# Dilation: the ScalarE place of the sign that makes each pattern

## The chip, the cores and the metric

The kernel runs on one core of a Trainium2 chip. The metric is the device time of the whole program in microseconds (us); the number given for a kernel is the median of several runs. Engines are named as the profile names them: PE is TensorE, DVE is VectorE, ACT is ScalarE, POOL is GpSimd, SP is the engine that issues most of the transfers.

## The reference, cut to what matters

Sixteen graphs of 1024 nodes with 128 features pass through two graph layers. Layer 0 is three times `h = hW + b; cos = nh nh^T; h = (adj * cos) h`. Layer 1 needs a thinned adjacency first, which is a sequential scan over the rows of each graph:

```python
def step(carry, n):
    row = carry[n]
    num = sum(row)
    sf = where(num > 10, (num + 1) // 2, 1)
    rank = cumsum(row)
    rm = row & (rank % sf == 0) & (mask[n] != 0) & (num > 1)
    carry = carry.at[n].set(row & ~rm)
    carry = carry.at[:, n].set(carry[:, n] & ~rm)
keep = scan(step, adj > 0);  adj_d = adj * keep
```

The kernel calls this scan "dilation". Three message-passing steps with batch statistics follow on `adj_d`, and do not concern the change.

## The kernel before, in words

The program has two halves in time. In the first (up to about 1530 us in the profile), layer 0 and the dilation run side by side; in the second, layer 1 runs.

**Layer 0** is a Python generator, `layer0()`. It issues small units of work and yields each unit's estimated PE time: `products` (PE products `pg` L344, multiplied on DVE by the adjacency into `ew`, L353 and L356), `turn` (PE transposes `gt` L373, copied back on ACT, L374), `sums` and `sums_back` (PE, L384 and L398), transposes of the adjacency (`pt_a` L260 on PE, copied by ACT into `adjA`, L261), features, squares for the norms (`hS` L319 on ACT), and so on.

**The dilation** works on blocks. A block `(k, half)` is one strip of 128 rows in eight of the sixteen graphs, so there are 16 blocks, done one after the other. Each block has three phases:

- `loads()`, once for each of the eight graphs `i`: SP brings a strip `an` of the adjacency (two buffers, L585); ACT makes the pattern, a row of ones and zeros in f16, with `Sign` (L587) and then `Relu` in place, which also sums the row (L588); DVE writes the left part of the pattern (L594) from `an` and from what was kept before. At every fourth graph PE transposes the four diagonal tiles (`pdt`, L608), ACT copies them (`dT`, L610), PE forms `pT` (L614 to L616) and ACT copies that into `T` (L618).
- `rounds()`: DVE starts with `Z` from `T` (L632 or L635), then alternates with PE some two to six times, and ends with ACT copying `E` (L722).
- `scans()`: DVE subtracts `E` from the patterns (L732); then for each graph DVE runs a scan of 1024 elements (L741) over the pattern, ACT takes an absolute value (`Abs`, L751), DVE compares (`kp`, L762), and POOL sends the row out (L763).

The patterns live in a ring `patt` of ten slots for blocks of eight. Pattern `i` of the next block, for `i` from 2 on, takes the slot of pattern `i-2` of the present block, and so may only be written when the scan of that pattern is over. Patterns 0 and 1 of the next block take the slots that the block before the present one used for its patterns 6 and 7.

**The code's order.** `dilation()` issues the loads of the next block among the scans of the present one: after each scan, one load. Every phase yields weights (0.8 a load, 2.5 a scan, 0.8 an `Abs`), and the driving loop issues layer-0 units in proportion until they have caught up, about 2 us of PE estimate for each unit of weight. In the code the order round scan `i` is therefore: scan `i`; layer-0 units; sign and relu `i` of the next block (and after `i` = 3 and 7 the `pdt`, `dT`, `pT`, `T` of its four graphs); layer-0 units; `Abs` `i-1`; layer-0 units; scan `i+1`.

**The order on an engine.** The framework that builds the program does not keep the code's order on an engine. It places instructions by its own estimate of when their operands are ready, so that an instruction may be put ahead of others that the code issued before it. `tc.keep_in_program_order(ins)` takes this away for one instruction: `ins` is not placed ahead of the last instruction that the code issued on the same engine before it. It adds no wait on hardware; it acts on the order of the queue alone. In the kernel before, the scans on DVE (L741) and the `Abs` on ACT (L751) are pinned in this way; the signs are not.

Of the kernel before, what the change touches and what calls it, by code (L numbers as in the profile page):

```python
# [11 lines left out]
AF = mybir.ActivationFunctionType  # L12
# [4 lines left out]
P = 128  # L17
# [29 lines left out]
def tile_adj_preln_d2(  # L47
# [40 lines left out]
    nc = tc.nc  # L88
# [111 lines left out]
    with ExitStack() as actx:  # L200
# [362 lines left out]
        def dilate(k, half, exact):  # L563
# [6 lines left out]
            def pattern(i):  # L570
                return patt[:, (at0 + i) % SLOTS, :]
# [9 lines left out]
            def loads():  # L581
                for i in range(BH):
                    b = half * BH + i
                    an = poold.tile([P, N], F32, tag="an", name=f"an{nk}_{i}")
                    nc.sync.dma_start(an, adj[b, cols, :])  # L585
                    on = pattern(i)[:, 2 + k * P :]
                    nc.scalar.activation(on, an[:, k * P :], AF.Sign)  # L587
                    nc.scalar.activation(on, on, AF.Relu, accum_out=rest[:, i : i + 1])  # L588
                    if k:
                        pk = poold.tile([P, NCH - 1, P], F16, tag="kl", name=f"kl{nk}_{i}")  # L590
                        nc.sync.dma_start(
                            pk[:, :k, :].rearrange("p j q -> p (j q)"), keep_d[b][: k * P, cols], transpose=True
                        )
                        nc.vector.scalar_tensor_tensor(  # L594
                            pattern(i)[:, 2 : 2 + k * P],
                            an[:, : k * P],
                            0.0,
                            pk[:, :k, :].rearrange("p j q -> p (j q)"),
                            ALU.is_gt,
                            ALU.mult,  # L600
                            accum_out=left[:, i : i + 1],
                        )
                    if i % GT == GT - 1:
                        four = range(i - GT + 1, i + 1)
                        bs_ = slice(i - GT + 1, i + 1)
                        pdt = ps_sm.tile([P, GT, P], F16, tag="sm", name=f"pdt{nk}_{i}")
                        for n, ii in enumerate(four):
                            nc.tensor.transpose(pdt[:, n, :], pattern(ii)[:, diag], ident16)  # L608
                        dT = poold.tile([P, GT, P], F16, tag="dT", bufs=1, name=f"dT{nk}_{i}")
                        nc.scalar.activation(dT, pdt, AF.Copy)  # L610
                        nc.vector.tensor_scalar(rbias[:, bs_], rest[:, bs_], 2.0, -2.0, ALU.mult, ALU.add)
                        pT = ps_sm.tile([P, GT, P], F32, tag="sm", name=f"pT{nk}_{i}")
                        for n, ii in enumerate(four):
                            nc.tensor.matmul(pT[:, n, :], lhsT=dT[:, n, :], rhs=upto, start=True, stop=False)  # L614
                            nc.tensor.matmul(pT[:, n, :], lhsT=pattern(ii)[:, diag], rhs=off, start=False, stop=False)
                            nc.tensor.matmul(pT[:, n, :], lhsT=ident16, rhs=after, start=False, stop=True)  # L616
                        for n, ii in enumerate(four):
                            nc.scalar.activation(T[:, ii, :], pT[:, n, :], AF.Identity, bias=rbias[:, ii : ii + 1])  # L618
                    yield 0.8
# [105 lines left out]
            def scans():  # L725
# [9 lines left out]
                for i in range(BH + 1):  # L735
# [28 lines left out]
                    yield False, 0.8  # L764

            return loads(), rounds(), scans()

        units0 = layer0()
# [448 lines left out]
```

## Time and profile before

| | |
|---|---|
| median of three runs | 2819.08 us (2816.39 to 2822.73) |
| the profiled execution | 2820.68 us |
| its span, first to last instruction | 2818.8 us |
| mean granted PE clock | 0.985 |
| busy in the span: PE, DVE, ACT, POOL | 2649.9, 1947.1, 1426.5, 477.6 us |
| sign L587 | 128 instructions, 293 / 686 / 1069 ns (least, median, most), from 17.1 to 1415.7 us |
| relu L588 | 128 instructions, 294 / 676 / 1082 ns, and 187 ns each for reading the sum |
| scan L741 | 128 instructions, 2282 ns (median), from 79.5 to 1511.1 us |
| last row of the dilation sent (L763) | 1521.3 us |

The span is divided at about 1530 us: before it, layer 0 and the dilation share the engines; after it comes layer 1. A "busy" figure counts the time in which an engine executed something; a wait is the idle time of an engine just before an instruction, with the instruction whose end allowed it to go on. Sizes differ between the signs because block `k` signs only the columns from `128k` on: 1024 elements a row at first, 128 in the last blocks.

### The profile page before, as it was taken

The page shows a single profiled execution, that of the slowest core. Times are in us where ns is not written, and L with a number is a line of the kernel's source. Part 1 is how long each engine was busy: PE and PEld are TensorE (multiplying, and loading weights), DVE is VectorE, ACT ScalarE, POOL GpSimd, SP SyncE. Part 2 cuts the span into 40 slices and gives each one's busy share as a digit, 9 for nine tenths or more (in the row PEclk, how much of TensorE's full clock was granted, in tenths as well). Part 3 has the DMA queues.
Part 4 walks back from the last instruction along what each step waited for, and adds up shares of the span by engine and source line. Part 5 has one row for each costly group of instructions (what it writes and reads, how often), then busy time and mean ns, then how long its engine had stood idle before and what let it go on. Part 6 is the DMA issues. An engine that isn't in the chain of part 4 may idle for free. (4 is left out here: it accounts for less than half of the span.)

```text
span 2818.8 us, 51980 instructions
## 1 busy us (share of the span) xinstructions
PE 2649.9 (94%) x18803; PEld 2193.2 (78%) x18803; DVE 1947.1 (69%) x4943; ACT 1426.5 (51%) x4097; POOL 477.6 (17%) x616
## 2 busy tenths in 40 slices
PE   6999999999999999999999999999989999999997
PEld 4666666676776676666676778888889999899997
DVE  3778778788888788889886467777762333456556
ACT  6757667558556566466454333343333334333334
POOL 3112112012012111121121012222220101010101
PEclk9999999999999999999999999999999999999999
DMA  8437347258366476386354069999976666576774
GB/s 283 135 128 241 99 159 240 75 159 245 85 201 173 101 226 186 95 254 182 93 178 162 1 234 386 402 402 387 402 297 214 203 216 201 188 238 228 234 237 135
DMA packets 382233, 585.22 MB, mean 208 GB/s; under 512 B 85200, under 2 KB 266448, under 8 KB 381968
## 3 DMA queue, kind: packets, MB, share of 16 engines
q1 hardware_dynamic: 343280, 425.28, 48.2%
q0 software_dynamic: 38688, 156.53, 14.8%
q8 instruction: 151, 2.47, 0.4%
q14 instruction: 114, 0.93, 0.1%
HBM read 403.44 MB, written 163.58 MB: 201 GB/s over the span
## 5 line engine op out<-in xcount | busy, mean ns | idle before, releaser
L890 PE MATMUL agg<-hw,aT 128*128 128x128 f32 (+1 forms) x6144 | 743.5, 277 | 8.2 <-DVE aT L995 7.3
L890 PEld LDWEIGHTS agg<-hw,aT 128*128 128x128 f32 x6144 | 713.4, 193 | 13.6 <-DVE aT L995 9.7
L344 PE MATMUL pg<-nhT 128*128 128x512 f32 (+3 forms) x1152 | 454.7, 497 | 40.4 <-DVE ew L356 39.1
L384 PE MATMUL po<-ew,hS 128*128 128x512 f32 (+3 forms) x1152 | 453.3, 497 | 8.1 <-ACT hTo L407 3.7
L356 DVE TENSOR_TENSOR ew<-pg,adjA 128x768 f32<-128x768 f32 (+3 forms) x528 | 423.6, 826 | 5.0 <-PE pg L344 5.0
L398 PEld LDWEIGHTS po<-ew,hS 128*128 128x128 f32 x2688 | 339.5, 193 | 39.1 <-issue 36.8
L398 PE MATMUL po<-ew,hS 128*128 128x128 f32 x2688 | 367.5, 277 | 1.2 <-ACT ew L374 1.2
L374 ACT ACTIVATE ew<-gt 128x512 f32<-128x512 f32 (+1 forms) x480 | 208.5, 464 | 245.3 <-PE gt L373 238.0
L741 DVE TENSOR_TENSOR_SCAN rank<-patt 128x1024 f16<-128x1024 f16 x128 | 294.9, 2305 | 0.1
L344 PEld LDWEIGHTS pg<-nhT 128*128 128x128 f32 x1152 | 187.9, 192 | 131.7 <-issue 89.3
L384 PEld LDWEIGHTS po<-ew,hS 128*128 128x128 f32 x1152 | 195.2, 193 | 99.8 <-issue 64.6
L373 PEld LDWEIGHTS gt<-ident,ew 128*128 128x128 f32 x1344 | 168.5, 143 | 100.7 <-issue 75.4
L373 PE MATMUL gt<-ident,ew 128*128 128x128 f32 x1344 | 212.3, 277 | 4.8 <-PEq L824 2.5
L948 POOL TENSOR_TENSOR o<-o,rn 128x512 f32<-128x512 f32 x93 | 108.5, 1167 | 638.3 <-DVE rn L942 627.6
L353 DVE TENSOR_TENSOR ew<-pg,adjA 128x128 f32<-128x128 f32 x384 | 108.1, 282 | 156.6 <-PE pg L344 117.3
L864 DVE TENSOR_TENSOR own<-pw,bs 128x256 f32<-128x256 f32 x192 | 81.4, 424 | 155.5 <-ACT hw L863 155.4
L862 PE MATMUL pw<-wrx,hT 128*128 128x256 f32 x768 | 179.7, 388 | 9.2 <-ACT hT L1065 8.4
L862 PEld LDWEIGHTS pw<-wrx,hT 128*128 128x128 f32 x768 | 145.1, 194 | 31.3 <-ACT hT L1065 9.2
L1013 ACT ACTIVATE aT<-pta 128x512 f32<-128x512 f32 (+3 forms) x160 | 71.3, 467 | 187.4 <-PE pta L1012 181.9
L751 ACT ACTIVATE rank<-rank,fin 128x1024 f16<-128x1024 f16 x128 | 146.7, 1151 | 36.3 <-DVE rank L741 35.6
L940 ACT ACTIVATE own<-o 128x128 f32<-128x128 f32 x378 | 112.7, 301 | 99.7 <-DVE o L919 99.5
L321 POOL TENSOR_TENSOR hS<-hN,rn 128x1024 f32<-128x1024 f32 x48 | 102.5, 2136 | 355.5 <-DVE rn L157 226.0
(169 smaller groups left out, 3930.6 us busy)
## 6 DMA issues: line engine op xcount, KB each, us to landing
an<-in_adj_dram SPq DMA_DIRECT2D x128, 512.0 KB, 4.3
keep<-kp POOLq DMA_DIRECT2D x128, 256.0 KB, 2.9
kb<-keep SPq DMA_DIRECT2D x128, 256.0 KB, 5.5
aT<-adT SPq DMA_DIRECT2D x32, 960.0 KB, 4.7
aT<-adT SPq DMA_DIRECT2D x32, 832.0 KB, 4.6
aT<-adT SPq DMA_DIRECT2D x32, 704.0 KB, 4.2
aT<-adT SPq DMA_DIRECT2D x32, 576.0 KB, 3.4
xb<-in_x_dram SPq DMA_DIRECT2D x31, 512.0 KB, 5.2
```

Source lines behind the costliest of these rows:

```text
L344: nc.tensor.matmul(pg[:, :n, :].rearrange("p c q -> p (c q)"), lhsT=self.nhT[:, q * P : (q + 1) * P], rhs=self.nhT[:, (q + c) * P : (q + c ...
L356: nc.vector.tensor_tensor(both[0][:, :, off, :], pg[:, own:n, :].unsqueeze(1).to_broadcast([P, 2, n - own, P]), both[1][:, :, off, :], ALU ...
L373: nc.tensor.transpose(pt[:, i, :], ew[:, at + i, :], ident)
L374: nc.scalar.activation(ew[:, at : at + n, :], pt[:, :n, :], AF.Copy)
L384: nc.tensor.matmul(self.po[:, c * P : (c + n) * P], lhsT=self.hS[:, q, :], rhs=ew[:, c - q : c - q + n, :].rearrange("p c q -> p (c q)"), ...
L398: nc.tensor.matmul(self.po[:, q * P : (q + 1) * P], lhsT=self.hS[:, q + n, :], rhs=ew[:, NCH - 1 - q + n, :], start=False, stop=closes and ...
L741: nc.vector.tensor_tensor_scan(rank, pt[:, 1 : N + 1], pt[:, 2:], 0.0, ALU.add, ALU.add)
L751: nc.scalar.activation(rank, rank, AF.Abs, bias=shift[:, i : i + 1], scale=1.0 if exact else -1.0)
L862: nc.tensor.matmul(pw[:, i, :], lhsT=hT[:, 2 * h + i, :], rhs=wrx[:, l, :], start=True, stop=True)
L890: nc.tensor.matmul(self.place(c), lhsT=aT[:, blk, :], rhs=self.hw[:, source, :], start=source == 0 and c % self.ga == 0, stop=ends(c, source),
L940: nc.scalar.activation(sq, o, AF.Square, accum_out=ss[:, c : c + 1])
L948: nc.gpsimd.tensor_tensor(self.o[:, hc, :], self.o[:, hc, :], rn.unsqueeze(2).to_broadcast([P, CPH, D]), ALU.mult)
```

## The change

One instruction is pinned: the `Sign` that makes a pattern. Nothing is computed differently, and no instruction is added or removed.

```diff
                     nc.sync.dma_start(an, adj[b, cols, :])
                     on = pattern(i)[:, 2 + k * P :]
-                    nc.scalar.activation(on, an[:, k * P :], AF.Sign)
+                    tc.keep_in_program_order(nc.scalar.activation(on, an[:, k * P :], AF.Sign))
                     nc.scalar.activation(on, on, AF.Relu, accum_out=rest[:, i : i + 1])
```

In the changed program a sign stands on ACT behind the ACT instruction that the code issued last before it: mostly a copy of a layer-0 unit (L374, L261), sometimes a square root (L155), the closing copy of a layer (L407) or the relu of the pattern before. The relu itself is not pinned, but reads what the sign wrote.

## The prediction

> **What bounds the kernel now.** I read the page first, then a table of busy time by stretch, the waits of ScalarE, the rows of the sign and of the transposes that read its pattern, and the timeline of one block. The dilation lies in the first 1525 us, so only that part can move. The busy time in it, and in two stretches of block 7, its scans (718 to 787) and the rounds after it (786 to 811), with columns PE, PEld, DVE, ACT, POOL:
>
> ```profile
> 70.00:1525.00 1455.00, 1373.47 (x8692) 1002.29 (x8690) 1200.24 (x2829) 904.79 (x2413) 254.57 (x317) 0.99 0.55 161
> ```
>
> ```profile
> 718.00:787.00 69.00, 66.21 (x387) 47.43 (x386) 56.26 (x104) 40.72 (x113) 9.05 (x9) 1.00 0.38 106
> ...
> 786.00:811.00 25.00, 24.53 (x185) 18.24 (x183) 22.17 (x62) 10.74 (x26) 2.17 (x4) 1.00 0.38 125
> ```
>
> PE is busy 94%, DVE 82%, ACT 62%. PE sets the pace; it loses 81.5 us in all there, and more of it in scans (2.8 of 69 us) than in rounds (0.5 of 25). ACT has room: what it idles costs only through those who wait for it. So what does ACT wait for, and who waits for its sign?
>
> ```profile
> ACT patt L587 <- DVE rank L741: 93.5, 73, 2.9
> ...
> ACT rank L751 <- DVE rank L741: 35.6, 20, 4.4
> ...
> ACT patt L587 <- DMA an<-in_adj_dram: 13.3, 6, 4.5
> ```
>
> ```profile
>   PEld pg L344: 2.1, 1
>   PE pt_a L260: 0.6, 1
> ```
>
> The first row is what the change is about: 73 of 128 signs stand at the head of ACT until a scan frees their slot, 93.5 us together. The second fence, the sign's own row, shows how little hangs on the sign directly: PE 0.6 us. Now the timeline from 768 to 789 us, block 7's last scans, with two signs, scan 7, a layer-0 copy, `pdt`, `dT`, and the start of the next rounds:
>
> ```profile
> 770.98 0.63 ACT L587 ACTIVATE patt<-an 128x512 f16<-128x512 f32 x1 [1.28 <-DVE rank L741]
> ...
> 777.37 2.28 DVE L741 TENSOR_TENSOR_SCAN rank<-patt 128x1024 f16<-128x1024 f16 x1
> ...
> 779.68 0.63 ACT L587 ACTIVATE patt<-an 128x512 f16<-128x512 f32 x1 [2.29 <-DVE rank L741]
> ...
> 780.98 0.47 ACT L374 ACTIVATE ew<-gt 128x384 f32<-128x384 f32 x1
> ...
> 782.98 0.39 PE L608 MATMUL pdt<-ident,patt 128*128 128x128 f16 x4
> ...
> 783.40 0.60 ACT L610 ACTIVATE dT<-pdt 128x512 f16<-128x512 f16 x1 [1.96 <-PE pdt L608]
> ...
> 786.11 1.22 DVE L635 TENSOR_SCALAR_CACHE_REDUCE Z<-T 128x1024 f16<-128x1024 f16 x1 [3.33 <-ACT T L618]
> ```
>
> Two things are to be seen. The signs at 770.98 and 779.68 come right behind scans 6 and 7: they are patterns 0 and 1 of block 9, issued a whole phase of rounds before their place in the code (after scan 0 of block 8, at 811). And `pdt`, which needs pattern 7 of block 8, runs only at 782.98, though that pattern's sign ran at 762.48: `pdt` keeps about its place in the code, behind scan 7, and the pattern waits 20 us for it. After it come `dT`, `T` and `Z` in one chain, for which DVE stands idle 3.33 us.
>
> **What the skill says.** "PSUM — Partial Sum Buffer", section Engine vs sequencer instructions: ScalarE's queue is strictly first in, first out, and TensorE's matmuls start and complete in program order. The trace agrees: nothing of ACT runs in the 2.29 us ahead of the sign at 779.68, though the copy L374 behind it follows within 1.3 us. Both ways of delay are in that sentence: a waiting sign blocks ACT, and a `pdt` that waits for a late pattern blocks PE. "ScalarE: Activation LUTs", section What ACT_TABLE_LOAD costs, gives an ACTIVATE with constant scale and bias 186 ns + 0.833 ns an element, 613 ns at 512; the trace has 630.
>
> **What the change moves.** It adds no work; 128 signs of 686 ns and, since they read them, 128 relus of 676 ns plus 187 ns move. Where to? I counted ACT's instructions in the code's order against their times in the trace; the one just before each sign in the code is the one that it will stand behind. 121 of the 128 signs move more than 5 us, with a median of 21.5 us, past a median of 22 ACT instructions; one predecessor was itself issued early, so that its pin holds nothing. Taking each predecessor at its present time, sign and relu then end at a time that can be set against the present start of their `pdt`. Over blocks 1 to 15 the median room is 25, 18, 8 us for patterns 0, 1, 2 and 26, 17, 7 for 4, 5, 6: none is late. For pattern 3 it is -1.7 us, late in 13 of 15; for pattern 7 it is -1.25, late in 14 of 15 by 22.3 us together. In the block shown: predecessor 780.98 + 0.47, then 0.63 + 0.63, makes 782.7, just in time. So early patterns only lose slack, but the fourth and eighth become the last thing before `pdt`.
>
> **What it costs and gives, step by step.**
>
> A. ACT's stalls go. I followed each wait of PE for ACT back along ACT's unbroken run of work to the wait it began with. Thirteen begin with a sign waiting for a scan: 8.3 us of PE. For DVE there are thirteen, 6.6 us; as PE has 5.6% idle and DVE is its main releaser, I count half, 3.3. The whole is 11.6; the signs still run on ACT among those copies, so I take two thirds: -8 us. Bounds: 0 (the next waiter takes over, such as `Abs` for its scan) and -16 (the `Abs` waits too, whose followers cost PE 7.7 us, shrink by half).
>
> B. PE at `pdt`. Today it never waits for the relu (0.2 us). The nearest row is the next link of the chain, where ACT's `dT` is also just ahead of PE: `pT` waits 8.1 us for `dT` over 32 groups. I take the same, +8. Bounds: 0, if PE is given other work meanwhile, and 27.7 + 22.3 = 50, the lateness of patterns 3 and 7, if PE stands for all of it.
>
> C. `T`, and so `Z`, comes later by pattern 7's lateness, 22.3 us over 15 blocks. In 11 of 16 blocks DVE already idles for `T` at `Z` (20.9 us), so 22.3 x 11/16 = 15 us more on DVE. PE is hardly idle in the rounds and only what reaches the next scans counts: 0.4 of it, +6. Bounds 0 and 15.
>
> D. The start. The first sign runs at 17.1 us; its predecessor, the square root L155, at 30.8. Strips `an` have two buffers, so the third strip is asked for only after sign 0, 14 us later. Signs 2 and 3 keep their times (35.0 and 41.3), as their predecessors end just before them; sign 4 moves from 47.6 behind a copy at 54.7 and its pattern is 2.4 us late for `pdt` at 54.9. I take +3, between 0 and +8 (sign 6's strip, which follows sign 4, must be fetched in a median of 4.3 us too). The sign that waits 4.54 us for its strip there hides nothing: PE waits for its own adjacency until 19.97.
>
> E. Nothing for the other queues. On SP the strips `an` wait 397.9 us for DVE's L594 and 43.6 us for ACT today; the predecessors of block 8's signs run from 715 to 781, some 9 us apart, and a strip is asked for two signs ahead and lands in 4.3 us, so before its sign. If that cover went, each late strip would block ACT as in D. POOL's rows leave after `kp`, which hangs on `Abs`; `Abs` already stands behind the relu's place in the code. DVE's L594 does not need the sign. The patterns pinned to the scans of the next block add two signs and relus, at most 4.7 us of ACT (1069 + 1082 + 187 ns, twice), to a scan phase where ACT idles 28 us of 69.
>
> Sum: -8 + 8 + 6 + 3 = +9 us on the profiled execution's 2820.7 (its span of 2818.8 and 1.9 around it), 2829.7; that execution lies 1.6 above the median, so 2828 against 2819.1.
>
> **Rivals.** (1) Faster: the head of ACT's queue is worth more than its direct waits. For it: DVE idles 55.1 us at `kp` behind a late `Abs`, and PE's idle lies in the scans, where the signs wait. Against: ACT catches up within a few us after most signs, waiting next for a transpose. With B to D near nothing and A at its bound with DVE in full (8.3 + 6.6), 2804. (2) The slack swallows both: ACT's 38% of idle pays for the stalls, and PE has other work at `pdt`; 2819, within 5. That the pin binds too little belongs here, but only 7 of 128 signs hardly move. (3) The dilation is the pacemaker after all: its chain of rounds and scans is serial, and 22.3 us of lateness, 8 at the start and B at 8 add in full, less 4 of A: +34, 2853. For it: DVE's idle at `Z`; against it: PE's 98% in rounds.
>
> **How the numbers follow.** My forecast, slower with 2822 to 2842 as its own range, has 0.43; rival 3 0.15; rival 1 0.30; rival 2 0.12. I take a change under 0.2%, 5.6 us, as not told from none. Rivals 1 and 3 stand on opposite sides and hold nearly half, so the range runs from just below 2804 to near 2853: 2802 to 2850, leaving out half of rival 3 and the tail of rival 1. Chances: slower 0.43 + 0.15 = 0.58, same 0.12, faster 0.30.
>
> **What would show it.** Right: the row of L587 waiting for L741 nearly gone; the first sign near 31 us; new waits of PE or PEld at L608 for the relu, 5 us or more; DVE's wait at `Z` for `T` grown from 20.9 to over 30; PE idle up by about 10 us before 1530. Wrong: no wait at L608 while PE's waits behind `adjA`, `hTo` and `kp` shrink, with the last row sent before 1521 (rival 1); PE's idle unchanged (rival 2); or the last row 25 us later and the second half shifted by as much (rival 3). A different order on PE or DVE, since a moved sign changes what else is ready when, could also outweigh every term here.

## The result, and the profile after

The changed kernel takes 2839.91 us (median of five runs, 2836.99 to 2851.71), the kernel before 2821.57 in the same five rounds. The ratio is 1.0078, 95% interval 1.0054 to 1.0101: slower, by about 18 us. The profiled execution of after took 2839.91 us, with a span of 2838.2.

First, where it lies. Busy time by stretch, cut in each kernel where the last row of the dilation is sent (columns as in the prediction, PE, PEld, DVE, ACT, POOL, then PE clock, DMA share, GB/s). Before:

```profile
0.00:1521.30 1521.30, 1415.03 (x8909) 1032.45 (x8910) 1221.82 (x2922) 948.33 (x2511) 275.55 (x362) 0.99 0.56 167
1521.30:2818.80 1297.50, 1234.90 (x9895) 1160.73 (x9894) 725.27 (x2023) 478.16 (x1586) 202.06 (x254) 0.98 0.72 256
```

After:

```profile
0.00:1541.00 1541.00, 1421.71 (x8909) 1035.85 (x8910) 1219.55 (x2922) 948.17 (x2511) 272.71 (x362) 0.98 0.54 165
1541.00:2838.20 1297.20, 1234.46 (x9895) 1160.76 (x9894) 724.57 (x2022) 478.42 (x1586) 201.68 (x254) 0.98 0.72 256
```

The second part is the same to 0.3 us; the first is 19.7 us longer with the same instructions. ACT and DVE work as long as before; PE is idle 13.0 us more (1541.00 - 1421.71 against 1521.30 - 1415.03) and busy 6.7 more.

What the change was about did go. The signs' row of after, with ScalarE's idle time before them, and no wait for a scan (93.5 us before):

```profile
its engine sat idle before it (us, times) until:
  DMA an<-in_adj_dram: 5.4, 2
```

Now the waits of PE, and of DVE, in the first 1545 us (who waited, for whom, total us, times, longest us). Four rows and what L594 waited for, before:

```profile
PE pg L344 <- DVE ew L356: 39.1, 37, 3.2
```

```profile
DVE ew L353 <- PE pg L344: 95.2, 86, 4.7
...
DVE Z L635 <- ACT T L618: 14.2, 8, 3.7
...
DVE rbias L611 <- ACT patt L588: 6.2, 7, 1.4
DVE patt L594 <- DMA kl<-keep: 5.9, 3, 2.9
```

After:

```profile
PE pg L344 <- DVE ew L356: 36.7, 41, 3.3
...
PE pc L673 <- DVE E L667: 9.0, 7, 3.9
PE pt_h L165 <- DVE x L421: 8.1, 7, 2.5
PE pdt L608 <- ACT patt L588: 8.0, 9, 3.6
```

```profile
DVE patt L594 <- DMA an<-in_adj_dram: 72.4, 39, 5.7
DVE ew L353 <- PE pg L344: 61.7, 67, 6.7
...
DVE rbias L611 <- ACT patt L588: 17.5, 13, 6.8
...
DVE Z L635 <- ACT T L618: 5.5, 3, 2.8
```

The first row of DVE is new: 39 times L594, which writes the left part of a pattern, stands at the head of DVE until its strip `an` lands, 72.4 us in all. Before there was no such row. (Ten more waits of L594, which the profile puts down to something else, also end within 0.1 us of the strip's landing; with them it is 82.8 us.) Part of it takes the place of other waits (`ew` for `pg` fell from 95.2 to 61.7), so that DVE's idle time, the stretch less the busy time in the tables above, grows by less: from 299.5 to 321.5.

Summed by who released PE, its waits up to the last row went so: DVE 56.3 to 71.2, DMA 16.6 to 20.6, ACT 29.0 to 23.4 (15.4 without the new row of `pdt`). The gain at ACT is there, and the longer waits for DVE outweigh it.

Why are strips late that landed in time before? The strip's own row in after, with its landing time (the last line: least, median, most):

```profile
who waited for it (us, times):
  DVE patt L594: 72.4, 39
  ACT patt L587: 5.4, 2
...
DMA to landing us min/median/max: 3.3/4.1/11.9
```

Before, the landing took 3.5/4.3/12.5 us, so the transfers themselves did not become slower. The strip has two buffers and two readers: ACT's sign takes its columns from `128k` on, DVE's L594 the columns left of that. A buffer is free when both are done. Over the 112 strips with a left part, set for the first two rows against the strip two before, the records give these medians:

| us | before | after |
|---|---|---|
| strip asked for, after L594 of two strips back ended | 0.08 | 13.70 |
| strip asked for, after the sign of two strips back ended | 1.50 | 0.03 |
| L594 starts, after its strip landed | 12.84 | 0.51 |
| sign starts, after its strip landed | 12.68 | 15.11 |

Before, the two readers ran close together, and L594 was mostly the later of them (75 of 110). After, the pinned sign frees the buffer, and L594, which is not pinned, has been placed as early as its operands were expected: some 14 us ahead of its own sign, right at the landing (54 of 112 start within 0.3 us of it). One case in block 5 of after, from its timeline (start, duration, instruction, and in brackets how long the engine stood and for what):

```profile
427.16 0.85 ACT L587 ACTIVATE patt<-an 128x768 f16<-128x768 f32 x1
...
428.15 1.05 SPq L585 DMA_DIRECT2D an<-in_adj_dram  x1
...
432.90 0.26 DVE L140 BATCH_NORM_STATS2 ln_st_l<-xb 128x6 f32<-128x128 f32 x1
...
435.66 0.42 DVE L594 SCALAR_TENSOR_TENSOR patt<-an,kl 128x256 f16<-128x256 f32 x1 [2.50 <-DMA an<-in_adj_dram]
...
436.01 0.18 DVE L141 BATCH_NORM_AGGREGATE ln_mv_l<-ln_st_l 128x2 f32<-128x6 f32 x1
...
436.54 3.18 ACT L148 ACTIVATE h<-x,ln_nmr_l,ln_rstd_l 128x128 f32<-128x128 f32 x8 [3.22 <-DVE ln_nmr_l L146]
437.29 0.68 DVE L297 TENSOR_TENSOR hN<-pw,b 128x512 f32<-128x512 f32 x1
...
438.02 0.33 PE L260 MATMUL pt_a<-ident,nat 128*128 128x128 f32 x1 [3.10 <-DVE hN L297]
```

The sign ends at 428.01, the strip for two loads later is asked for at 428.15, and its L594 stands 2.50 us at the head of DVE. What stood behind it, a norm and `hN`, has nothing to do with strips: L141 reads what DVE's own L140 had finished by 433.16, and yet starts at 436.01. ACT then stands 3.22 us and PE 3.10. The same strip in before: the sign waits for a scan, L594 waits for nothing, both start together, and the next strip is asked for 0.03 us after the later of them, here the sign.

```profile
427.78 0.84 ACT L587 ACTIVATE patt<-an 128x768 f16<-128x768 f32 x1 [0.83 <-DVE rank L741]
427.79 0.42 DVE L594 SCALAR_TENSOR_TENSOR patt<-an,kl 128x256 f16<-128x256 f32 x1
...
428.65 0.34 SPq L585 DMA_DIRECT2D an<-in_adj_dram  x1
```

### The profile page after: what moved, and what is told of

Read it like the earlier page. It is cut to its first block, busy times and chain, and to the rows that moved or that the text cites. A ratio compares the mean times of both kernels' runs of the same rounds, so it can differ in the third digit from the quotient of the medians.

```text
span 2838.2 us, 51958 instructions
## 1 busy us (share of the span) xinstructions
PE 2656.2 (94%) x18803; PEld 2196.6 (77%) x18803; DVE 1944.1 (68%) x4943; ACT 1426.6 (50%) x4097; POOL 474.4 (17%) x616
## 5 line engine op out<-in xcount | busy, mean ns | idle before, releaser
L890 PEld LDWEIGHTS agg<-hw,aT 128*128 128x128 f32 x6144 | 713.2, 192 | 13.6 <-DVE aT L995 9.7
L344 PE MATMUL pg<-nhT 128*128 128x512 f32 (+3 forms) x1152 | 455.1, 498 | 42.2 <-DVE ew L356 36.7
L374 ACT ACTIVATE ew<-gt 128x512 f32<-128x512 f32 (+1 forms) x480 | 210.7, 467 | 279.3 <-PE gt L373 277.9
L741 DVE TENSOR_TENSOR_SCAN rank<-patt 128x1024 f16<-128x1024 f16 x128 | 294.6, 2302 | 0.2
L373 PEld LDWEIGHTS gt<-ident,ew 128*128 128x128 f32 x1344 | 167.3, 142 | 98.8 <-issue 72.9
L373 PE MATMUL gt<-ident,ew 128*128 128x128 f32 x1344 | 211.8, 275 | 3.2 <-PEq L824 2.7
L1013 ACT ACTIVATE aT<-pta 128x512 f32<-128x512 f32 (+3 forms) x160 | 71.2, 466 | 188.0 <-PE pta L1012 175.9
L319 ACT ACTIVATE hS<-hN 128x128 f32<-128x128 f32 x384 | 114.4, 301 | 96.0 <-DVE hN L303 85.8
L763 POOL DMA_DIRECT2D keep<-kp x128 | 70.7, 553 | 547.7 <-DVE kp L762 473.6
```

The source lines that it names most:

```text
L319: nc.scalar.activation(hS[:, c, :], self.hN[:, c, :], AF.Square, accum_out=ss[:, c : c + 1])
L344: nc.tensor.matmul(pg[:, :n, :].rearrange("p c q -> p (c q)"), lhsT=self.nhT[:, q * P : (q + 1) * P], rhs=self.nhT[:, (q + c) * P : (q + c ...
L373: nc.tensor.transpose(pt[:, i, :], ew[:, at + i, :], ident)
L374: nc.scalar.activation(ew[:, at : at + n, :], pt[:, :n, :], AF.Copy)
L741: nc.vector.tensor_tensor_scan(rank, pt[:, 1 : N + 1], pt[:, 2:], 0.0, ALU.add, ALU.add)
L890: nc.tensor.matmul(self.place(c), lhsT=aT[:, blk, :], rhs=self.hw[:, source, :], start=source == 0 and c % self.ga == 0, stop=ends(c, source),
```

## The experiments

Two theories. **Theory S** (strips): the later sign holds a strip buffer, the unpinned L594 runs into the landing, and DVE stands there. **Theory P** (late patterns): patterns 3 and 7 now come just before or after their `pdt`, and the waits of PE at `pdt` and of DVE at `rbias` (6.2 us before, 17.5 after) make the loss. The kernel before ran beside each group of kernels: 2819.33 us beside the first four, 2820.92 beside the next four, 2820.79 beside the last. All ratios are against it, with their 95% interval.

### Three strip buffers, with and without the pin

```diff
-                    an = poold.tile([P, N], F32, tag="an", name=f"an{nk}_{i}")
+                    an = poold.tile([P, N], F32, tag="an", bufs=3, name=f"an{nk}_{i}")
...
-                Z = poold.tile([P, BH, P], F16, tag="Z", name=f"Z{nk}")
+                Z = poold.tile([P, BH, P], F16, tag="Z", bufs=1, name=f"Z{nk}")
...
-                E = poold.tile([P, BH, P], F16, tag="E", name=f"E{nk}")
+                E = poold.tile([P, BH, P], F16, tag="E", bufs=1, name=f"E{nk}")
```

`Z` and `E` give up a buffer to make room. The same edit went onto the changed kernel and, as control, onto the kernel before.

> The changed kernel with a third buffer for the strips an (room from one buffer instead of two for Z and E). Theory S (strips): the pinned sign keeps its strip some 14 us longer, so the strip two further on is asked for late and DVE's L594 stands for its landing (72.4 us in 39 waits). With a third buffer that row falls below 15 us and most of the loss goes: 2815 to 2827. Theory P (transposes): the loss is pdt waiting for the late patterns 3 and 7 and the chain behind it; a third strip leaves it, 2835 to 2845, and the wait of L608 for L588 stays near 22 us (PE and PEld together).

> Control: the kernel before with the same three strip buffers and single Z and E. Both theories: within 6 us of the kernel before, 2815 to 2827, since its strips land 12.8 us (median) before L594 already. If it moves more, the buffers themselves do something, and the third strip's effect under the pin must be read against this run.

Changed kernel with three strips: 2807.19 us, ratio 0.9956 (0.9940 to 0.9973). Kernel before with three: 2816.80, 0.9991 (0.9984 to 0.9998). The buffer is worth about 33 us to the changed kernel and some 3 to the kernel before. The waits of DVE's L594 in the changed kernel with three strips:

```profile
DVE patt L594 <- DMA an<-in_adj_dram: 13.8, 7, 3.6
```

From 72.4 us to 13.8 (82.8 to 21.0 with the waits that the profile names otherwise), with L594 now a median of 3.5 us behind the landing. With the buffer the pin is a gain. S's row came out as expected; the time is below the ranges of both theories, so more than the loss came back. `pdt` still waits 4.4 us for its pattern, `rbias` 11.4. In the control, whose patterns are early and whose time is not longer, `rbias` waits 12.3 us too: that row alone is no sign of a loss.

### Both readers pinned, and L594 alone

```diff
-                        nc.vector.scalar_tensor_tensor(
-                            pattern(i)[:, 2 : 2 + k * P],
...
+                        tc.keep_in_program_order(
+                            nc.vector.scalar_tensor_tensor(
+                                pattern(i)[:, 2 : 2 + k * P],
...
```

Both signs and L594 pinned, then L594 alone with the signs free as before.

> The changed kernel with DVE's L594, which makes the left part of a pattern from the same strip, pinned on DVE too, so that it is not put ahead of where the code has it. Theory S: L594 no longer stands for strips (row below 15 us), and the time comes back to 2815 to 2828. Theory P: unchanged, 2835 to 2845.

> Control: the kernel before with L594 alone pinned on DVE. Here the strip is held by L594 instead of by the sign, and the sign, not pinned, is the one that may stand for a landing, on ACT. Theory S: if strips are what costs, ACT's waits of L587 for strips grow from 13.3 us towards 60, but ACT has room: 2818 to 2830. Theory P: the patterns are early as before, so no loss: 2815 to 2825.

Both pinned: 2792.32 us, 0.9905 (0.9888 to 0.9921), well below what either theory said. No L594 waits for a strip any more, as S had it; it starts a median of 12.6 us after the landing. The late patterns stay. PE's waits with both pinned (line numbers are two higher below the edit):

```profile
PE pt_a L260 <- DMA nat<-in_adj_dram: 21.2, 8, 7.0
PE pg L344 <- DVE ew L356: 15.4, 23, 1.8
PE pdt L610 <- ACT patt L588: 7.0, 8, 3.0
```

`pdt` waits 7.0 us, about as in after (8.0), and `rbias` 13.1; yet the kernel is 47 us faster than after. So P's waits alone do not make a kernel slow; what they cost is not settled by this. That this kernel also beats before goes with the second row: PE waits for `ew` 15.4 us, where it was 39.1 in before and 36.7 in after.

L594 alone pinned: 2840.79 us, 1.0078 (1.0061 to 1.0095), as slow as after, where S had 2818 to 2830. ScalarE's waits in that kernel:

```profile
ACT patt L587 <- DMA an<-in_adj_dram: 186.2, 76, 6.6
ACT ew L374 <- PE gt L373: 166.0, 118, 5.4
```

It is the mirror image: now L594 frees the buffer (the strip is asked for 0.07 us after its end, 13.8 us after the sign's), and the free sign floats to the landing, 83 of 112 within 0.3 us of it. ACT stands 186.2 us for strips, far more than the 60 expected, and its spare time did not cover it: PE's waits for ACT are 55.2 us here, 29.0 in before. What stands behind the sign in ACT's queue is late for PE. It is what "PSUM — Partial Sum Buffer", section Engine vs sequencer instructions, in the Trainium skill lets one expect of a queue that is strictly first in, first out, and the expectation priced only the waiting instruction and not the queue.

### Half of the signs

```diff
-                    nc.scalar.activation(on, an[:, k * P :], AF.Sign)
+                    sign = nc.scalar.activation(on, an[:, k * P :], AF.Sign)
+                    if i % GT == GT - 1:
+                        tc.keep_in_program_order(sign)
```

This pins signs 3 and 7 alone, the late ones; its counterpart has `i % GT < GT - 1` and pins the other six of each block.

> The kernel before with the sign pinned for the fourth and eighth graph of a block alone (i = 3 and 7), the two whose pattern is the last thing before pdt. Theory S (strips): only two of eight strips are held long, so DVE's L594 waits some 18 of 72 us and the time is 2818 to 2830. Theory P (transposes): these two signs carry the whole loss, 2832 to 2845, with L608 waiting for L588 near 22 us (PE and PEld).

> The other six signs of each block pinned, i = 3 and 7 left free. Theory S: most strips are still held, L594 waits 40 us or more and the time is 2827 to 2842. Theory P: pdt's patterns are early again (L608 waits under 5 us) and the loss is gone, 2812 to 2824.

Signs 3 and 7: 2836.80 us, 1.0058 (1.0041 to 1.0074), where S had 2818 to 2830. L594 waits only 7.0 us for strips there (11.3 with those named otherwise), ACT's signs still wait 58.1 for scans, and the waits that P names are 5.7 at `pdt` and 16.6 at `rbias`. In 29 of 32 groups a relu ends less than 1 us ahead of the group's last `pdt`, in after in 24, in before in 4. The time is a miss of S and within P's 2832 to 2845, and `pdt` with its weight loads waits 20.5 us, near P's 22. So it speaks for P as a second cost, with most of the gain at ACT missing. It does not show it: the new waits of late patterns are 16.1 us, and those for strips, with the signs' own on ACT (13.3 to 19.3), about as much. (Its profiled execution, 2829.68, is at the low end of its runs, so its profile shows only some 9 us of the loss.)

The other six: 2830.90 us, 1.0035 (1.0017 to 1.0052), with 43.3 us at L594 for strips; the time and the row are as S expected. Three quarters of the signs bring over half of S's wait. ACT's signs stand 38.9 us for strips as well, 33.6 of them for the strips of the two signs left free. The patterns are early (a relu within 1 us of the last `pdt` in 3 of 32 groups), and there is a loss all the same, against P's 2812 to 2824; `pdt` still waits 6.4 us, but in two places. The two halves add up to 0.93% and the whole is 0.78%, which these intervals do not tell apart.

### The best of both, and the early six with L594

Both readers pinned with three strip buffers; and L594 pinned with the early six signs only.

> Sign and L594 both pinned, and three strip buffers. Theory S: with L594 pinned no strip is waited for any more, so the third buffer adds little: 2782 to 2796, against 2792 for both pins with two buffers. Theory P: the same.

> L594 pinned, and the sign pinned but for i = 3 and 7. Theory S: nothing to gain from strips; sign 3 and 7, free again, may stand for a strip on ACT: 2788 to 2800. Theory P: what is left of the cost at pdt (PE waits 7.0 us there with both pins) goes: 2782 to 2788.

Both pinned with three strips: 2785.65 us, 0.9873 (0.9846 to 0.9901). It has the lowest median, 1.3% below the kernel before and 1.9% below the changed one, and within the range of both theories. The first part of its span ends at 1482.3 us:

```profile
0.00:1482.30 1482.30, 1403.00 (x8909) 1024.15 (x8910) 1219.96 (x2922) 947.73 (x2511) 272.83 (x362) 1.00 0.57 171
```

PE is idle 79.3 us of it, against 106.3 in before. L594 with the early six signs: 2802.94 us, 0.9942 (0.9924 to 0.9960), a smaller gain than with all eight, and above both expected ranges. ACT stands 53.8 us for strips in it, against 4.9 with all pinned; 48.0 of them are for the strips of the two free signs, 3 and 7, the place that S had named.

### Loads issued one place earlier

```diff
+                if loads:
+                    yield next(loads)
                 for scanned, weight in this:
                     yield weight
                     if scanned and loads:
-                        yield next(loads)
+                        got = next(loads, None)
+                        if got:
+                            yield got
```

The first load of the next block is issued ahead of scan 0, and with it each later load moves one scan forward. `pdt` is issued inside the fourth and the eighth load, so it moves forward with its patterns. The edit was put on the changed kernel, on the one with both readers pinned, and on the best version.

> The changed kernel (sign pinned) with each load issued one scan earlier in the code: the first load of the next block ahead of scan 0, the next one after scan 0, and so on. The patterns 3 and 7 then come about 8 us before their pdt. Theory S (strips): L594 still floats to the landing of a strip that the sign holds, so its wait stays above 40 us and the time at 2828 to 2842. Theory P (late patterns, at pdt and at rbias L611): the waits of L608 and L611 fall under 5 us each and the time comes to 2812 to 2826.

> Sign and L594 pinned, loads one scan earlier. Theory S: little is left to gain, 2786 to 2796 against 2792 without the earlier loads. Theory P: what the pin costs at pdt (7.0 us of PE) and at rbias (13.2 us of DVE) goes, 2775 to 2786.

> The same with three strip buffers, which gave 2786 with the loads in their old place. Theory S: 2780 to 2790. Theory P: 2768 to 2780.

On the changed kernel: 2822.35 us, 1.0009 (0.9998 to 1.0019), so the whole loss is gone. The reason is not the one that P would give. DVE's waits there (lines four higher below the edits):

```profile
DVE rbias L615 <- ACT patt L592: 19.5, 12, 6.9
...
DVE patt L598 <- issue: 12.2, 4, 5.3
DVE patt L598 <- DMA an<-in_adj_dram: 11.4, 7, 3.3
```

The waits of P are as in after (`pdt` 7.2, `rbias` 19.5), while the strips fell from 72.4 to 11.4 us. The row "issue", for which the profile names no releaser, ends 0.1 us after the strip's landing each time; with all such waits the fall is from 82.8 to 24.4. Neither theory had forecast this pair, S having expected the strips to stay above 40; why they fell is open. But the two are separated: with P's waits unchanged and S's down to less than a third, the time is that of before. Two things limit this. The gain at ACT is still there (its signs wait 5.5 us for scans), so it may pay for a cost of P; and the same edit on the kernel before was not tried. (Its profiled execution, 2827.68, is the longest of its twelve.)

With both pinned the earlier loads change nothing that the intervals tell apart (2796.51, 0.9919, 0.9897 to 0.9941, against 0.9905), nor on the best version (2791.83, 0.9898, 0.9881 to 0.9914, against 0.9873); both are just above S's ranges and far from P's. `pdt` and `rbias` did not shrink there either (7.4 and 18.8; 5.2 and 15.6): against their own `pdt` the patterns come no earlier, and no run here has removed P's waits.

### A third buffer for the mirror image

Three strips with L594 pinned and the signs free.

> L594 alone pinned (2841 with two strip buffers, with ACT standing 186 us for strips at the sign), now with three. Theory S: the loss is the strip that the pinned reader holds while the other reader waits for the next, so a third buffer takes the wait under 60 us and the time to 2795 to 2815. Against it: if the order of DVE alone made the loss, 2832 to 2845.

2861.61 us, 1.0142 (1.0126 to 1.0159), the slowest of all and far from the 2795 to 2815 expected. ScalarE's waits in it:

```profile
ACT ew L374 <- PE gt L373: 149.2, 105, 5.4
ACT patt L587 <- DMA an<-in_adj_dram: 131.2, 48, 5.2
...
ACT patt L587 <- DVE rank L743: 47.6, 31, 3.3
```

"Perfetto Trace Analysis" in the Trainium skill, section Identifying Performance Opportunities, says that gaps that repeat can mean too few buffers. That agreed with the changed kernel (33 us for one buffer) and does not here, where ACT's 186.2 us for strips fell to 131.2 only: the free sign floated again to the landing, a median of 0.5 us behind it, and where the strip no longer holds it, it stands for the scan. Here the reader that is placed as early as it can be used up the room. Why it is slower than with two buffers is open.

## Why the prediction was right, and where not

It forecast 2828 us, slower; it came out slower, 18.3 us by the paired medians and 19.2 by the profiled executions, against +9. The direction was right, but half of the reason was not. Of the five signs of being right that it named, four came: the row of L587 waiting for L741, the first sign, the waits at L608 (22.0 us on PE and its weight loads), PE's idle time (13.0 us more). The fifth, `Z`, did not.

**A, ACT's stalls, -8 of 0 to -16.** Right. The signs' waits for scans are gone (93.5 to 0), those of `Abs` too (35.6 to 0), and PE's waits for ACT without the new ones fell from 29.0 to 15.4 us. Of these 13.6, 6.3 lie at `pT` behind `dT` (8.1 to 1.8), the next link after `pdt` and not a stall of A; that leaves 7.3, close to the value taken.

**B, PE at `pdt`, +8.** The row came out as priced, 8.0 us in 9 waits, but the 6.3 us saved at `pT` stand against it: the wait has in the main moved one link forward. What the step left out is the other reader of the same pattern: `rbias` on DVE, L611, also needs the relu, and went from 6.2 to 17.5 us. The kernel with signs 3 and 7 pinned speaks for a cost of late patterns; no run took these waits alone away, so their share of the loss stays open.

**C, a later `Z`, +6.** Wrong in its sign. DVE's wait at `Z` for `T` fell from 20.9 to 8.6 us, where over 30 was forecast. DVE now waits before `Z` already, at `rbias` and at the strips, which would take the place of that wait; that was not tried by itself.

**D, the start, +3.** The first sign runs at 29.3 us (near 31 forecast), but the first scan starts at 79.9 against 79.5. Nearly nothing is left by then.

**E, "Nothing for the other queues", 0.** This is the step that failed. Its sentences were that a strip "lands in 4.3 us, so before its sign" and "DVE's L594 does not need the sign". Neither is the point. The strip does land before its sign, by a median of 15 us; but L594 reads the same strip, it is not pinned, and it was placed at the landing. L594 needs no result of the sign but it needs the buffer that an earlier sign holds. Priced at 0, it measured 72.4 us of DVE's waits, and PE's waits for DVE rose by 14.9. The prediction named the trap for ACT ("each late strip would block ACT") and did not ask the same of the second reader.

The sum at PE, by the releasers named above: -13.6 (ACT), +8.0 (`pdt`), +14.9 (DVE, in which what `rbias` and the strips cost PE is contained, not told apart), +4.0 (DMA, `nat`), and +6.7 of busy time make 20.0, against the 19.7 us by which the last row was later. A and B as measured make -5.6, and C and D gave nothing: without the cost that it had put at nothing, the kernel would have come out faster by these terms. That "slower" came true is in good part luck.

One reading of a line was wrong too. For the queue that is first in, first out, the prediction named the copy L374 behind the sign at 779.68; but PE's L373 wrote what that copy reads from 780.07 on, so it could not have run earlier anyway. Another place in before shows it: the sign waits for its strip, and the copy behind it, whose input PE had ended at 485.00, runs only after the sign.

```profile
484.51 0.49 PE L373 MATMUL gt<-ident,ew 128*128 128x128 f32 x3
...
486.13 0.74 ACT L587 ACTIVATE patt<-an 128x640 f16<-128x640 f32 x1 [1.28 <-DMA an<-in_adj_dram]
...
486.78 0.47 ACT L374 ACTIVATE ew<-gt 128x384 f32<-128x384 f32 x1
```

**The rivals.** That ACT's queue is worth more (faster, 2804) was not what happened, though with a third strip buffer the changed kernel takes 2807, which agrees with a gain of that size behind the strips. That slack swallows both is out. The pacemaker (2853) would have had the last row 25 us later; it came 19.7 later, but by another mechanism. The last sentence of the prediction, that a different order on DVE could outweigh every term, was the nearest to it.

What stays open: why pinning L594 lowers PE's waits for `ew`. In the kernels with L594 and all or some signs pinned they are 14.9 to 21.4 us, with L594 alone 22.9 (31.5 with three buffers), in those without 29.5 to 40.9. The pattern is plain, the chain behind it was not traced. Open too are the share of the late patterns in the loss, and the 6.7 us by which PE is busier in after. Each edit also changes the order in which the framework places other instructions, so the gains are not those of the strips alone: both pins, and the pin with three strips, gained more than the loss.

## What to carry to other kernels

Before pinning or delaying an instruction, list every buffer that it reads and every other reader of that buffer on another engine: here the later reader set when the next transfer started, and the reader left free to float stood for the landing at the head of its queue. Pin both or neither; here pinning either one cost 0.78%, both gained 0.95%, and with one more buffer 1.27%. A third buffer paid here where the waiting reader was DVE's and not where it was ACT's, so try it on the version meant, not on its control.

## What was not expected of the hardware

The same 8909 matmuls of the first part are busy for 1402.3 to 1421.7 us in the profiled executions of these kernels, the granted clock being 0.98 in after and 1.00 in the two best orders with three strips. Not all of this need be the order. Twenty runs of one kernel, before with three strips, had a granted clock between 0.986 and 0.990 over the whole span: at 0.990 they took 2810.9 to 2813.7 us, at 0.986 2820.1 and 2821.9. The execution of it that was profiled is one of the fastest (2811.9) and has PE busy for 1405.7 us, where before has 1415.0 at nearly the same idle time of PE (107.1 and 106.3). "Perfetto Trace Analysis" in the Trainium skill, section Matmul Optimizations, states that the matmul engine scales its power with its utilization; whether the clock follows the order in that way no run here shows. So a difference of some 10 us in PE's busy time between two single executions, in a profile that models the ends of matmuls, should not be explained by a change of order, and the 6.7 us of after are within that.

And the landing time of a strip reaches 11.9 us at a median of 4.1 in after (12.5 and 4.3 in before). A reader that starts a median of 12.8 us behind the landing, as L594 did in before, never waited for it; one placed a median of half a microsecond behind it meets that spread, with 39 late strips at 1.9 us each on average.
